# Layer 0 of a graph attention stack: putting a group's neighbour lists in order of rank on TensorE instead of through indirect transfers

## The chip, the cores and the metric

The kernel runs on one core of one Trainium2 chip. The metric is the device time of one execution in microseconds. The kernel before was run nine times; the median is 3138.7 us. The profile that the text reads is a single further execution.

## The reference

There are 3327 nodes of 256 features and a symmetric adjacency matrix with about 1% of its entries set, the diagonal included. Four layers follow one another. Each is "attention over the neighbours, added to the input, then normalised"; they differ in how the score of an edge is made. Layer 0 is the one that the change touches:

```python
g_src = nodes @ W_src_w.T + W_src_b
g_tgt = nodes @ W_tgt_w.T + W_tgt_b
g = jax.nn.leaky_relu(g_src[:, None, :] + g_tgt[None, :, :], 0.2)
score = jnp.where(adj_mat != 0, jnp.einsum('ijc,c->ij', g, a_w), -jnp.inf)
weights = jax.nn.softmax(score, axis=1)
x = layernorm(x + weights @ g_tgt)
```

Its score does not factorise: each edge needs 256 values of its own. Layers 1 to 3 have scores that are a sum of a row term and a column term, and are computed densely.

## The kernel before, in words

**Layer 0** (`sparse0`) works on the edges alone. The rows are cut into 26 tiles of 128, and the tiles into three groups of 5, 9 and 12 (`SETS`). A first stage (`targets`, lines 360 to 372) multiplies all rows with the target weights on TensorE (PE) and writes them to `table_d` in HBM, one table row per node. Beside it, and later beside the gathers, the generator `neighbours(s)` (lines 399 to 516) makes for every row of group s a list of its neighbours' table rows:

- per tile, two halves of the adjacency rows are loaded (`adj_i`, two buffers used in turn), and L425 multiplies "is an edge" with the column's number (`rev`, which holds 4096 plus the column). L448 takes the eight largest of every 104 columns, and L467 and L469 sort up to 56 of them into `found`. The tile's `payload` has 58 columns: 56 table rows, the node's own number in the group, and a mark for the diagonal.
- a key per row (number of neighbours, own number) is laid on a diagonal (L499) and spread over all partitions by a product with ones (L500, into the PSUM tile tagged "keys"). When the group's tiles are done, L509 counts for every row the keys that are larger. That is the row's rank in the group, between 0 and 128 times the group's tiles; L513 makes integers of it.

The rows of a group are then put in order of rank, so that the rows with most neighbours lie together and a tile of short rows needs fewer gathers (`LEVELS`: 56, 38, 34, 32 and 28 for the first group's five tiles). `write_list(s, t)` does this: an indirect transfer on POOL (L522) writes the 128 payloads of tile t to the places in `lists_d` that their ranks name. After the last tile `read_lists(s)` (L530) reads the list back as `lst`, where partition p of tile t holds the row of rank 128 t + p.

**The gathers.** For each sorted tile, POOL issues one indirect transfer for the nodes' own rows (L555, from `own_d`) and one per neighbour place (L563, from `table_d`), in parts of eight; a part goes into one of eleven buffers, four parts ahead of its use. DVE takes the maximum with the negated source row (L582) and sums the weighted result (L588); ACT scales the gathered rows (L669), PE adds them up (L672). L708 on POOL puts the finished rows back to their places in HBM.

**What sets the order.** In `sparse0`, PE, DVE, ACT and POOL execute in the order in which the program is written. SP's loads are not in that order: the framework's scheduler places each where it expects its buffer to be free, so loads of a later step can be issued ahead. Group 0's `neighbours` runs beside the first stage to its end; then come group 0's five `write_list`, its `read_lists`, and the loop over parts q. In this loop the `neighbours` generators of groups 1 and 2 are advanced by as many steps as their due times ask for, ahead of `score(q)` on DVE. Their list writes are put into a queue (`between`) from which POOL takes one after every second gather.

**Layers 1 to 3** (`layers`) are dense products of edge weights with features, bounded by PE. Layer 1 starts when the last group's rows are back. If some row had more neighbours than the lists hold, a flag (`lost`) would run a dense version of everything; with these inputs it does not run.

Of the kernel before, what the change touches and what calls it, by code (L numbers as in the profile page):

```python
# [8 lines left out]
F32 = mybir.dt.float32  # L9
BF16 = mybir.dt.bfloat16  # L10
I32 = mybir.dt.int32
U32 = mybir.dt.uint32
U16 = mybir.dt.uint16
AF = mybir.ActivationFunctionType
ALU = mybir.AluOpType
# [4 lines left out]
P = 128  # L20
BANK = 512
# [6 lines left out]
KMAX = 56  # L28
CHUNK = 104
FIRST = 3  # L30
BASE = 4096


SETS = (5, 9, 12)
# [13 lines left out]
def gat_stack(  # L48
# [29 lines left out]
    nc = tc.nc  # L78
    n, dim = x.shape
# [189 lines left out]
    def sparse0(lost):  # L269
        GROUP, TURNS, LEAD = 8, 11, 4  # L270
        starts = [sum(SETS[:s]) for s in range(len(SETS))]
        with ExitStack() as s0:
            const0 = s0.enter_context(tc.tile_pool(name="s_const", bufs=1))
            io0 = s0.enter_context(tc.tile_pool(name="s_io", bufs=2))
            gath = s0.enter_context(tc.tile_pool(name="gath", bufs=1))
            ps0 = s0.enter_context(tc.tile_pool(name="s_ps", bufs=2, space=PSUM))
# [21 lines left out]
            for c in range(kc):  # L298
                t = io0.tile([P, dim], F32, tag="minus", name="dots0")
# [9 lines left out]
            rev = const0.tile([P, nt * P], U16, name="rev")  # L309
# [9 lines left out]
            own_i = const0.tile([P, nt], U32, name="own_i")  # L319
# [5 lines left out]
            own_f = const0.tile([P, nt], F32, name="own_f")  # L325
# [70 lines left out]
            len_c = nt * P // CHUNK  # L396
            assert all((-(-hi // P) * P - lo) % CHUNK == 0 for lo, hi in halves)

            def neighbours(s):

                size = SETS[s]
                keys = io0.tile([P, max(SETS)], F32, tag="keys", name="keys")
                ranks = io0.tile([P, max(SETS)], F32, tag="ranks", name="ranks")
                ranks_i = io0.tile([P, max(SETS)], U32, tag="ranks_i", name="ranks_i")
                key_rows = ps0.tile([P, max(SETS) * P], F32, tag="keys", name="key_rows", bufs=1)
                payloads = []
                of_rows = iter(())
                for t in range(size):
                    it = starts[s] + t
# [6 lines left out]
                    for b, (lo, hi) in enumerate(halves):  # L416
                        w, padded = hi - lo, -(-(hi - lo) // P) * P
                        adj_i = io0.tile([P, nt * P // 2], I32, tag="adj_i", name="adj_i")
# [4 lines left out]
                        elif w < padded:  # L423
# [3 lines left out]
                            op0=ALU.not_equal, op1=ALU.mult, accum_out=sums[:pn, b : b + 1],  # L427
# [38 lines left out]
                    for r in range(0, KMAX, 8):  # L466
# [8 lines left out]
                        sums[:, 3:4], found, axis=AX.X, op=ALU.add, negate=True  # L475
                    )
                    nc.vector.tensor_reduce(lost[:, it : it + 1], sums, axis=AX.X, op=ALU.add)
                    payload = io0.tile([P, KMAX + 2], U32, tag=f"pay{t}", name="payload", bufs=1)
                    nc.vector.tensor_scalar(
                        payload[:, :KMAX], found, 1.0 - BASE, 0.0, op0=ALU.add, op1=ALU.max  # L480
                    )
                    nc.vector.tensor_copy(payload[:, KMAX : KMAX + 1], own_i[:, it : it + 1])
                    nc.vector.tensor_scalar_mul(
                        payload[:, KMAX + 1 :], sums[:, 2:3], -1.0
                    )
# [10 lines left out]
                        op0=ALU.mult, op1=ALU.subtract,  # L496
                    )
                    key_diag = io0.tile([P, P], F32, tag="key_diag", name="key_diag")
# [8 lines left out]
                for t in range(size):  # L507
# [3 lines left out]
                        op0=ALU.is_gt, op1=ALU.add, accum_out=ranks[:, t : t + 1],  # L511
                    )
                nc.vector.tensor_copy(ranks_i[:, :size], ranks[:, :size])  # L513
                placed[s] = ranks_i, payloads
                yield

            placed = {}
            listed = {}

            def write_list(s, t):  # L520
                ranks_i, payloads = placed[s]
                nc.gpsimd.indirect_dma_start(  # L522
                    out=lists_d[s][:, :],
                    out_offset=bass.IndirectOffsetOnAxis(ap=ranks_i[:, t : t + 1], axis=0),
                    in_=payloads[t][:, :], in_offset=None,
                )

            def read_lists(s):
                lst = io0.tile([P, max(SETS), KMAX + 2], U32, tag="lst", name="lst")
                nc.gpsimd.dma_start(  # L530
                    lst[:, : SETS[s], :], lists_d[s].rearrange("(t p) k -> p t k", p=P)
                )
                listed[s] = lst
# [3 lines left out]
            places = {key: LEVELS[SETS[key[0]]][key[1]] for key in tiles}  # L537
# [286 lines left out]


            first = neighbours(0)
            for it in range(nt):
                for _ in targets(it):
# [29 lines left out]
            at = begins[len(SETS) - 1]  # L858
# [3 lines left out]
            for s in range(len(SETS) - 1):  # L862
# [2 lines left out]
                    at_step(at + 2, project_next, it)  # L865
                    at += 3
                at = max(at, begins[len(SETS) - 1] + 19)
            for it in range(SETS[0]):
                write_list(0, it)
            read_lists(0)  # L870
            for s in range(1, len(SETS)):
                lo, hi = starts[s] * P, min(n, (starts[s] + SETS[s]) * P)
                copy_rows(nc.sync, own_d[s][: hi - lo, dim : 2 * dim], x[lo:hi, :])
# [3 lines left out]
            for s in range(1, len(SETS)):  # L877
                at = begins[s] - LEAD - 1
                at_step(at, read_lists, s)
                at -= SETS[s] // 4 + 1  # L880
                for it in range(SETS[s]):
                    at_step(at, between.append, lambda s=s, it=it: write_list(s, it))
                ahead.append(neighbours(s))
                steps += 6 * SETS[s] + 3
                owed[at] = steps
# [732 lines left out]
    lost = nodes.tile([P, 2 * nt], F32, name="lost")  # L1618
    nc.vector.memset(lost, 0.0)
    rest = sparse0(lost)  # L1620
    with ExitStack() as rs:
        layers(rs, EARLY, rest)
# [75 lines left out]
```

## Time and profile before

| what | us |
|---|---|
| median of nine runs (lowest, highest) | 3138.7 (3134.86, 3143.18) |
| the profiled execution's own time | 3136.12 |
| its span, first to last instruction | 3134.3 |
| first stage and group 0's ranks (to 128.8) | 128.8 |
| from there to DVE's second y operation (165.2) | 36.4 |
| from there to the end of group 1's ranks (404.6) | 239.4 |
| from there to the last put-back on POOL (1494.9) | 1090.3 |
| layers 1 to 3 (to 3134.3) | 1639.4 |

Over the whole span PE is busy 71%, DVE 72%, ACT 24%, POOL 33% of the time. From 165.2 to 404.6 us, DVE is busy for 230.9 of 239.4 us and POOL for 170.7; from 404.6 to the last gather at 1467.3, POOL for 808.7 of 1062.7 and DVE for 787.6.

A row in order of time has: start and duration in us, engine, line, operation, output<-inputs, and in brackets the idle time of the engine ahead of it with what ended it. A row of waits has: engine, what waited, its line, <- what it waited for: us in total, how many times, the longest. A group's row has: busy us, mean ns of one | idle us just before, and its releasers. "L522" is line 522 of the kernel before. [...]

### The profile page before, as it was taken

To read this page: it belongs to the slowest core of one execution; us is meant where nothing else is said; L and a number is where in the kernel's file an instruction comes from. 1 tells how busy PE (TensorE), PEld (TensorE's weight loads), DVE (VectorE), ACT (ScalarE), POOL (GpSimd) and SP (SyncE) were. 2 spreads that over 40 slices of the span, in tenths; PEclk is the share of its full clock that TensorE was granted. 3 is DMA by queue.
4 is the path that set the end of the run, shared out by engine and by line. 5 is a ranking of instruction groups with operands and counts; after the bars stand their busy time and mean duration, and the time that the engine had idled before them with its cause. 6 is when DMAs were issued, how large, how long until landed. Compare 5 with 4: busy or idle time off the path is not lost.

```text
span 3134.3 us, 44325 instructions
## 1 busy us (share of the span) xinstructions
PE 2230.1 (71%) x15676; PEld 1261.4 (40%) x15676; DVE 2260.1 (72%) x6075; ACT 750.0 (24%) x2094; POOL 1039.5 (33%) x1053
## 2 busy tenths in 40 slices
PE   7514342452443554344789999999999999999997
PEld 3302121221211221122668888884434545444332
DVE  7589999999956555554445542108888899899997
ACT  0003231432333344333234421110110110110110
POOL 0177767777777777775000000000000000000000
PEclk9998676676766776677999999999999999999998
DMA  7566546555435544443766753332212212212211
GB/s 222 155 145 188 169 124 166 171 159 150 114 101 113 133 112 117 119 116 88 226 180 201 208 151 92 105 104 73 68 45 70 68 47 69 68 45 60 56 47 47
DMA packets 179448, 367.64 MB, mean 117 GB/s; under 512 B 34294, under 2 KB 125608, under 8 KB 178194
## 3 DMA queue, kind: packets, MB, share of 16 engines
q1 hardware_dynamic: 98248, 174.31, 19.7%
q0 software_dynamic: 50688, 154.27, 18.9%
q10 hardware_dynamic: 30282, 36.15, 3.3%
q8 instruction: 126, 2.06, 0.3%
q14 instruction: 104, 0.85, 0.1%
HBM read 322.58 MB, written 45.43 MB: 117 GB/s over the span
## 4 chain that ended last, share of the span: by engine, by line
PE 45%; DVE 4%; DMA 2%; issue 1%; ACT 0%; POOL 0%; SPq 0%; DVEq 0%; POOLq 0%; ACTq 0%
PE acc L1353 17%; PE acc L1306 15%; PE acc L1361 8%; DVE e L1222 3%; PE misc L1152 3%; DMA at_i<-in_adj_t_dram 1%; DMA at<-at_d 1%; PE misc L1249 0%; PE misc L1435 0%; PE misc L1396 0%; DVE stats L1513 0%; DVE h L248 0%; DVE h L1511 0%; DVE h L1326 0%; DVE both L1508 0%
## 5 line engine op out<-in xcount | busy, mean ns | idle before, releaser
L563 POOL DMA_INDIRECT g<-table_d,lst x923 | 916.8, 993 | 281.7 <-issue 266.6
L1222 DVE SCALAR_TENSOR_TENSOR e<-rate,feat,at 128x896 f32<-128x896 f32 (+4 forms) x832 | 844.1, 1081 | 81.4 <-PE acc L1361 69.7
L672 PE MATMUL acc<-g,ident 128*128 128x512 f32 (+1 forms) x934 | 453.4, 643 | 433.8 <-ACT g L669 402.6
L1353 PE MATMUL acc<-e,feat 128*32 128x384 f32 (+2 forms) x6656 | 690.2, 516 | 7.5 <-DVE h L1326 4.8
L672 PEld LDWEIGHTS acc<-g,ident 128*128 128x128 f32 x934 | 193.2, 211 | 667.0 <-ACT g L669 445.7
L582 DVE TENSOR_TENSOR y<-g,both 128x1024 f32<-128x1024 f32 (+2 forms) x240 | 275.7, 1174 | 202.6 <-DMA g<-table_d,lst 200.3
L1353 PEld LDWEIGHTS acc<-e,feat 128*32 128x32 f32 x6656 | 258.4, 110 | 347.9 <-issue 236.0
L1361 PE MATMUL acc<-e,feat 128*32 128x384 f32 (+3 forms) x3328 | 376.0, 512 | 0.0
L669 ACT ACTIVATE g<-g,w 128x256 f32<-128x256 f32 x923 | 370.6, 493 | 0.0
L588 DVE SCALAR_TENSOR_TENSOR y<-y,both 128x256 f32<-128x256 f32 x923 | 324.7, 417 | 0.0
L1306 PE MATMUL acc<-feat,e 128*128 128x257 f32 (+2 forms) x1352 | 308.7, 384 | 21.4 <-DMA feat<-feats_d 13.3
L1306 PEld LDWEIGHTS acc<-feat,e 128*128 128x128 f32 (+2 forms) x1352 | 255.8, 192 | 63.1 <-issue 14.3
L242 POOL TENSOR_TENSOR rstds<-rstds,minus_half 128x7 f32<-128x7 f32 (+1 forms) x12 | 19.8, 1649 | 755.6 <-DVE rstds L241 755.6
L1306 PE MATMUL acc<-feat,at 128*128 128x257 bf16 (+2 forms) x2028 | 237.8, 274 | 5.2 <-DMA at<-at_d 4.9
L500 PE MATMUL key_rows<-key_diag,ones 128*128 128x128 f32 x52 | 18.0, 445 | 288.1 <-DVE key_diag L499 239.5
L1306 PEld LDWEIGHTS <-at 128*128 128x128 bf16 (+2 forms) x2028 | 198.7, 99 | 39.0 <-DMA at<-at_d 5.5
L1361 PEld LDWEIGHTS acc<-e,feat 128*32 128x32 f32 (+1 forms) x3328 | 139.0, 110 | 154.8 <-issue 131.2
L1222 DVE SCALAR_TENSOR_TENSOR e<-rate,feat,at_i 128x896 f32<-128x896 f32 (+2 forms) x104 | 111.3, 1080 | 95.8 <-ACT feat L1160 54.3
L1202 POOL DMA_DIRECT2D rate3b_d<-rate_rows x4 | 2.1, 520 | 468.0 <-ACT rate_rows L1201 468.0
L448 DVE MAX8 cand<-num 128x8 f32<-128x104 uint16 x832 | 145.6, 251 | 1.0
L500 PEld LDWEIGHTS key_rows<-key_diag,ones 128*128 128x128 f32 x52 | 11.9, 278 | 301.6 <-DVE key_diag L499 223.2
L1239 ACT CAST at<-at_i 128x896 bf16<-128x896 int32 (+2 forms) x104 | 92.0, 885 | 98.6 <-DMA at_i<-in_adj_t_dram 70.7
(182 smaller groups left out, 1758.5 us busy)
## 6 DMA issues: line engine op xcount, KB each, us to landing
at<-at_d SPq DMA_DIRECT2D x150, 224.0 KB, 2.5
at_i<-in_adj_t_dram SPq DMA_DIRECT2D x50, 448.0 KB, 4.9
adj_i<-in_adj_dram SPq DMA_DIRECT2D x25, 832.0 KB, 4.6
adj_i<-in_adj_dram SPq DMA_DIRECT2D x25, 831.5 KB, 5.3
g<-table_d,lst POOLq DMA_INDIRECT x923, 2.8
at<-at_d SPq DMA_DIRECT2D x75, 192.0 KB, 2.4
at<-at_d SPq DMA_DIRECT2D x75, 191.8 KB, 2.3
at_d<-at ACTq DMA_DIRECT2D x50, 224.0 KB, 4.1
```

The costliest lines, as they stand in the source:

```text
L448: nc.vector.max(cand[:, lo // CHUNK + c, :], spread_v[:, c, :, :])
L563: nc.gpsimd.indirect_dma_start(out=g[:, k - k0, :], out_offset=None, in_=table_d[:, :], in_offset=bass.IndirectOffsetOnAxis(ap=entry["lst" ...
L582: nc.vector.tensor_tensor(y, rows, minus_src[:, None, :].to_broadcast([P, m, dim]), op=ALU.max)
L588: nc.vector.scalar_tensor_tensor(y, y, 1.0, a, op0=ALU.mult, op1=ALU.mult, accum_out=sc)
L669: nc.scalar.activation(rows, rows, AF.Copy, scale=w[:, k : k + 1])
L672: nc.tensor.matmul(dst, ident, rows, start=start, stop=stop)
L1152: nc.tensor.matmul(pacc[:pn, : dim + self.extra], ht[:, k, :pn], self.weight[:, k, :], start=(k == 0), stop=(k == kc - 1),)
L1222: nc.vector.scalar_tensor_tensor(e[:pn, : c1 - c0], self.rate[b][:pn, h_of, : c1 - c0], q, at[:pn, : c1 - c0], op0=ALU.max, op1=ALU.mult,)
L1239: nc.scalar.copy(at[:pn, :w], at_i[:pn, :w])
L1306: nc.tensor.matmul(accs[s][:pn, : dim + 1], a[:pj, s * P : s * P + pn], f[:pj, : dim + 1], start=(j == 0 and part == 0), stop=(j == nt - 1 ...
L1353: nc.tensor.matmul(accs[x][p][q : q + 32, : hi - lo], f[:pj, at0 : at0 + 32], es[at0 // hd][:pj, lo:hi], start=(j == 0), stop=(j == nt - 1),)
L1361: nc.tensor.matmul(accs[x][pairs][h_of * 32 : (h_of + 1) * 32, : hi - lo], f[:pj, dim + h_of : dim + h_of + 1].to_broadcast([pj, 32]), es[ ...
```

## The change

For group 0 alone, the sorted list is made on chip. `neighbours(0)` calls a new function, `permute`, behind the rank count; the five L522 transfers of group 0 and their L530 read are gone. Groups 1 and 2 keep theirs. The payloads of group 0 are float32 instead of uint32.

`permute` splits every rank into a tile number (rank shifted right by 7) and a row (rank minus 128 times that), and adds 4096 to both, so that they can be compared with `rev`. For each of the five tiles it makes a 128x128 matrix with a 1 where the row's place is the column ("unit"), a 5-wide mark of the tile ("pick"), and the payload repeated five times and multiplied with the mark ("moving", 5 x 58 = 290 columns, in the buffers tagged "adj_i"). A product of unit and moving, added up over the five tiles in one PSUM bank (tagged "keys"), has the list in order of rank; one copy makes integers of it.

```diff
+            placed = {}
+            listed = {}
+
             def neighbours(s):
...
-                    payload = io0.tile([P, KMAX + 2], U32, tag=f"pay{t}", name="payload", bufs=1)
+                    payload = io0.tile(
+                        [P, KMAX + 2], U32 if s else F32, tag=f"pay{t}", name="payload", bufs=1
+                    )
...
-                    nc.vector.tensor_copy(payload[:, KMAX : KMAX + 1], own_i[:, it : it + 1])
+                    nc.vector.tensor_copy(payload[:, KMAX : KMAX + 1], own_f[:, it : it + 1])
...
                 nc.vector.tensor_copy(ranks_i[:, :size], ranks[:, :size])
                 placed[s] = ranks_i, payloads
+                if s == 0:
+                    permute(size, ranks, ranks_i, payloads)
                 yield
 
-            placed = {}
-            listed = {}
+            def permute(size, ranks, ranks_i, payloads):
+
+
+                at = io0.tile([P, 2, max(SETS)], F32, tag="places", name="places", bufs=1)
+                tile_i, tile_f, row_f = ranks_i[:, :size], at[:, 0, :size], at[:, 1, :size]
+                nc.vector.tensor_scalar(
+                    tile_i, tile_i, 7, None, op0=ALU.logical_shift_right
+                )
+                nc.vector.tensor_copy(tile_f, tile_i)
+                nc.vector.scalar_tensor_tensor(
+                    row_f, tile_f, -float(P), ranks[:, :size], op0=ALU.mult, op1=ALU.add
+                )
+
+                nc.vector.tensor_scalar(
+                    at[:, :, :size], at[:, :, :size], float(BASE), None, op0=ALU.add
+                )
+                cols = size * (KMAX + 2)
+                assert cols <= BANK and n >= P
+                sorted_ps = ps0.tile([P, max(SETS) * P], F32, tag="keys", name="sorted", bufs=1)
+                for t in range(size):
+                    unit = io0.tile([P, P], F32, tag="key_diag", name="unit")
+                    nc.vector.tensor_scalar(
+                        unit, rev[:, :P], row_f[:, t : t + 1], None, op0=ALU.is_equal
+                    )
+                    pick = io0.tile([P, max(SETS)], F32, tag="keys", name="pick")
+                    nc.vector.tensor_scalar(
+                        pick[:, :size], rev[:, :size], tile_f[:, t : t + 1], None, op0=ALU.is_equal
+                    )
+                    moving = io0.tile(
+                        [P, size, KMAX + 2], F32, tag="adj_i", name="moving"
+                    )
+                    nc.vector.tensor_tensor(
+                        moving, payloads[t][:, None, :].to_broadcast([P, size, KMAX + 2]),
+                        pick[:, :size, None].to_broadcast([P, size, KMAX + 2]), op=ALU.mult,
+                    )
+                    nc.tensor.matmul(
+                        sorted_ps[:, :cols], unit, moving.rearrange("p t k -> p (t k)"),
+                        start=(t == 0), stop=(t == size - 1),
+                    )
+                lst = io0.tile([P, max(SETS), KMAX + 2], U32, tag="lst", name="lst")
+                nc.vector.tensor_copy(
+                    lst[:, :size, :].rearrange("p t k -> p (t k)"), sorted_ps[:, :cols]
+                )
+                listed[0] = lst
...
                 at = max(at, begins[len(SETS) - 1] + 19)
-            for it in range(SETS[0]):
-                write_list(0, it)
-            read_lists(0)
             for s in range(1, len(SETS)):
                 lo, hi = starts[s] * P, min(n, (starts[s] + SETS[s]) * P)
```

## The prediction, on record before the result

> **What bounds the kernel now.** I read the page's costliest groups first, then the waits of POOL and DVE over the whole run, then both engines' rows in order of time around the change.
>
> ```profile
> L563 POOL DMA_INDIRECT g<-table_d,lst x923 | 916.8, 993 | 281.7 <-issue 266.6
> ```
>
> Layer 0 is a stream of 923 gathers on POOL. Busy and idle together are some 1,200 us of the 1,314 between the first gather (153.5 us) and the last (1467.3), and the idle time is issue (0.30 us ahead of each). So the time of layer 0 is when the stream starts, plus its length, plus whatever stops it. Two of POOL's waits over the whole run name what stops it:
>
> ```profile
> POOL lists_d L522 <- DVE ranks_i L513: 123.9, 1, 123.9
> ...
> POOL lists_d L522 <- DVE lost L610: 20.3, 1, 20.3
> POOL lists_d L522 <- DMA lists_d<-payload,ranks_i: 14.9, 6, 4.3
> ```
>
> The first is the start (group 0 has to be ranked). The second is a stop in mid-stream. In order of time, POOL at both places:
>
> ```profile
> 129.19 2.43 POOL L522 DMA_INDIRECT lists_d<-payload,ranks_i  x1 [123.86 <-DVE ranks_i L513]
> 135.61 1.09 POOL L522 DMA_INDIRECT lists_d<-payload,ranks_i  x1 [3.99 <-DMA lists_d<-payload,ranks_i]
> ...
> 148.34 0.93 POOL L530 DMA_DIRECT2D lst<-lists_d  x1 [1.53 <-DMA lists_d<-payload,ranks_i]
> 152.22 1.00 POOL L555 DMA_INDIRECT own_of<-own_d,lst  x1 [2.94 <-DMA lst<-lists_d]
> ...
> 162.28 0.94 POOL L563 DMA_INDIRECT g<-table_d,lst  x1 [0.30 <-issue]
> ...
> 404.85 0.98 POOL L522 DMA_INDIRECT lists_d<-payload,ranks_i  x1 [20.26 <-DVE lost L610]
> ```
>
> The six transfers to be removed fill 129.19 to 152.22. But at 404.85 POOL has stood still for 20.26 us, waiting for group 1's ranks from DVE. Whatever POOL gains before that point is lost there, unless DVE is earlier too. So DVE's stretch from group 0's ranks (128.72) to group 1's (404.40) decides:
>
> ```profile
> 128.72 0.17 DVE L513 CAST ranks_i<-ranks 128x5 uint32<-128x5 f32 x1
> 128.80 1.88 DVE L425 SCALAR_TENSOR_TENSOR num<-adj_i,rev 128x1664 uint16<-128x1664 int32 x1
> ...
> 156.94 0.42 DVE L582 TENSOR_TENSOR y_own<-own_of,both 128x256 f32<-128x256 f32 x1 [18.26 <-ACT both L579]
> ...
> 160.24 1.22 DVE L582 TENSOR_TENSOR y<-g,both 128x1024 f32<-128x1024 f32 x1 [2.82 <-DMA g<-table_d,lst]
> 165.17 1.22 DVE L582 TENSOR_TENSOR y<-g,both 128x1024 f32<-128x1024 f32 x1 [3.71 <-DMA g<-table_d,lst]
> ...
> 404.40 0.17 DVE L513 CAST ranks_i<-ranks 128x9 uint32<-128x9 f32 x1
> ```
>
> DVE does the first tile of group 1 at once (128.80 to 138.69), then waits 18.26 + 2.82 + 3.71 = 24.8 us for the first gathers, all of it before 165.17. From 165.17 to 404.40 the list of DVE's waits is empty. So what the change is worth is how much earlier the row at 165.17 comes. After 404.85 nothing stops POOL until its last rows, and the next layer begins with its last one (1492.49).
>
> One more thing is seen in time: a gather caught by L425 is stretched.
>
> ```profile
> 203.35 2.44 POOL L563 DMA_INDIRECT g<-table_d,lst  x1 [0.30 <-issue]
> ```
>
> L425 ran on DVE from 203.09 to 204.98, and the gather ended 0.8 us later. All 41 POOL transfers over 1.4 us lie beside one of the 42 L425 rows after 128 us in this way.
>
> **What the Trainium skill says.** "SBUF — State Buffer", section "Who interferes with whom": a DVE instruction with two SBUF inputs holds the port pair that it shares with GpSimd. L425 reads adj_i and rev from SBUF; the trace agrees (0.95 us becomes 2.44). "DMA: Bandwidth & Descriptors", section "Anatomy of one DMA": about 2 us of a transfer are fixed, most of it the receipt of the write. The list writes landed after 2.2 us (median), though the first took over 4 beside two adjacency loads. "TensorE: Matmul & The Clock Gate", section "What's actually happening": an idle array starts at half clock. Here four 128x256 instructions take 1.91 us after 48.89 us of idling as after 3.41, so my price, taken from these rows, holds that already. For the widened multiply see the next part.
>
> **The change, part by part.**
>
> *Removed*: five L522 writes, the L530 read. POOL's 129.19 to 152.22 (23.0 us) is free.
>
> *Added before the first product* (DVE): shift, cast, fused multiply-add, base added: four small ones, dependent, 0.19 us apart as L463 and L464 are: from 128.91 to 129.67. Then the unit matrix (128x128, as L499: 0.29, next one after 0.21), the pick (128x5) and the product with it, which waits some 0.19 for the pick. This last, 128x290 with two SBUF inputs, the trace does not have; "VectorE: DVE Perf Modes", section "The TRN2 errata", gives (N+151)/0.96 ns, so 0.46 us as an estimate (the same formula gives 1.22 for 128x1024, and the row above has 1.22). The first product can start at about 130.65.
>
> *Added on PE*: five f32 products of 290 columns, two instructions each. Instructions of 128 columns start 0.28 us apart, of 256 0.46 to 0.50, of 260 0.51; carried on to 290 columns 0.51 to 0.56, so 1.02 to 1.13 for a product, and I take 1.1. DVE needs 0.8 for the next tile's three operations, so PE sets the pace: 5.5 us and 0.2 to drain, end 136.35. Bounds: 0.8 (DVE's pace) and 1.5 us (double the 674 ns mean of L351's 260 columns, and a tenth more): the end moves by -1.5 to +2.
>
> *Copy of the sorted list* from PSUM: L509 took 0.88 for 640 columns, so 0.5 for 290: 136.9. POOL starts 0.3 later, as at 129.19: **own_of at 137.2 instead of 152.22, 15.0 earlier.** Late next could be own_d and table_d, which the gathers read: their last writes are issued at 120.79 and 117.63 and land in 2.6 us (median), before 137. No wait there.
>
> *Moved: group 1's first adjacency loads.* The moving tiles take the two "adj_i" buffers in turn, five uses after ten loads and two index rows. So the loads for tile 0 of group 1, which SP had issued at 109.72 and 119.68, wait for the fourth and fifth product: issued at about 135.35 and 136.4. Such a load landed 5.3 us after its issue at 77.40, so the first is there at 140.65; the second, even at twice that, before 147. Behind them on SP are only loads that are later still. DVE's first tile, which had run from 128.80, now runs at 140.65, 3.7 us after the copy; its halves take 5.17 and 4.72: 150.54. Then y_own, y at 151.1, and the second y could go at 152.3.
>
> *The gathers meanwhile*: 1.25 us each from 137.2, but both L425 rows (140.65 and 145.85) now catch one, and cost about 1.5 each: the ninth POOL transfer (at 162.28 before) starts at 137.2 + 8 x 1.25 + 2.9 = 150.1, and as before 2.89 us pass until DVE's second y: **153.0 instead of 165.17, 12.2 earlier**. By DVE alone 12.9. If the loads were not late, the collisions would come earlier and the gathers would still say about 153. So the two limits lie close together, and 12.2 is what I take.
>
> *Cost at nothing*: 20 DVE and 10 PE instructions, covered by time in which both stood idle; without that cover 8 us, what is between 128.8 and 136.9. The payload's type and its own-number copy: same shapes.
>
> *After that*: DVE's stretch to 404.40 holds no wait, so group 1's ranks come 12.2 earlier; POOL arrives earlier too, waits its 20 us, and goes on from the same event, so their relative places afterwards are the same. Sum: 3136.1 (profiled execution; span 3134.3) - 12.2 = 3123.9. The median of the nine is 3138.7, 2.6 above that execution: **3138.7 - 12.2 = 3126.5**.
>
> **The rivals.** (a) *The lead is swallowed*: POOL's 20.26 us wait simply grows to 35, time 3138.7. For: it is on the same engine, and DVE is busy throughout before it. Against: the 24.8 us that DVE waits before 165.17 are in the same stretch. (b) *Adjacency late*: SP takes a column load (xt) first, which waits for the products behind the sorting ones on PE (some 3 us), and the two loads share the way with the gathers, 2 us more: 7 us gained, 3131.7. For: the first stage moves 209 GB/s; against: SP has served such loads by readiness. (c) *Slower*: after 404.85 POOL is the bound and 24 of its transfers are caught by L425, 23.2 us in all, 0.97 each (0.54 to 1.70 by row). If the new phase made them all 1.70, 17.6 us would be added: 3144.1. It decides from 12.2/24 more, 1.48 a piece. Against: both engines start again from one event. (d) *The list is late anyway*, because products with 290 columns take twice what I take: 5.5 later, 3132.0.
>
> **How the numbers follow.** Forecast 0.74 (3122 to 3130), (a) 0.07, (b) and (d) together 0.12, (c) 0.07. Range 3122 to 3133: the first case and most of (b) and (d). A measurement of this kernel can tell some 0.2% from no change, 6.3 us: 3132.4 to 3145.0. Faster 0.82 (the first case and two thirds of (b) and (d)), same 0.12, slower 0.06 (what lies beyond (c)).
>
> **What would show it.** Right: own_of at about 137 on POOL; the first L425 of group 1 waiting for adj_i until about 141; the second y at about 153; then no DVE wait until ranks at 392; POOL's L522 wait still about 20 us; its last row near 1480. Wrong: a DVE wait between 153 and 392; products over 1.3 us; a stop on POOL after 392; or a changed length of the layers after 1495 (1,639 us).

## The result, and the profile after

The kernel with the change takes 3126.88 us (median of nine runs, 3123.07 to 3130.82). The kernel before took 3138.7 in the same comparison (29 runs, 3134.51 to 3143.18): ratio 0.9963, 95% interval 0.9955 to 0.9971, so 11.8 us less. The forecast was 3126.5. The profiled execution of after took 3123.54 (span 3121.6), against 3136.12 (3134.3) of before: 12.7 us less in the span. Lines are those of after from here on: 49 more than before behind the new function (L522 is L571, L555 is L604, L563 is L612, L582 is L631), three to five more ahead of it (L425 is L428, L513 is L518).

The profile's costliest group and, from POOL's waits over the whole run, the two that take the place of the two shown of before:

```profile
L612 POOL DMA_INDIRECT g<-table_d,lst x923 | 923.7, 1001 | 283.1 <-issue 263.1
```

```profile
POOL own_of L604 <- DVE lst L564: 131.7, 1, 131.7
...
POOL lists_d L571 <- DVE lost L659: 17.8, 1, 17.8
```

The stream of 923 gathers is still the bulk of layer 0. (A gather's row on POOL is not its transfer: it takes 1.0 us on the mean, while the data land 2.8 us after the issue.) What released the stream's start is now the copy of the sorted list on DVE, at 137 us. The wait for group 1's ranks is still there, 17.8 us instead of 20.3. POOL in order of time at these places, and at its last put-back:

```profile
137.02 1.06 POOL L604 DMA_INDIRECT own_of<-own_d,lst  x1 [131.70 <-DVE lst L564]
138.38 0.98 POOL L612 DMA_INDIRECT g<-table_d,lst  x1 [0.30 <-issue]
139.67 2.59 POOL L612 DMA_INDIRECT g<-table_d,lst  x1 [0.30 <-issue]
...
145.08 2.35 POOL L612 DMA_INDIRECT g<-table_d,lst  x1 [0.30 <-issue]
...
392.88 0.99 POOL L571 DMA_INDIRECT lists_d<-payload,ranks_i  x1 [17.76 <-DVE lost L659]
...
1483.49 0.97 POOL L757 DMA_INDIRECT sums_d<-hs,lst  x1 [17.87 <-DVE hs L750]
```

The last put-back of the kernel before:

```profile
1492.49 0.97 POOL L708 DMA_INDIRECT sums_d<-hs,lst  x1 [17.38 <-DVE hs L701]
```

There are three different gains: `own_of` starts 15.2 us earlier than before (152.22), group 1's first write 12.0 earlier (404.85), the last put-back 9.0 earlier (1492.49). The two rows of 2.59 and 2.35 us are gathers caught by L428 (the rows at 139.53 and 144.71 below). DVE in the same stretch:

```profile
128.70 0.17 DVE L518 CAST ranks_i<-ranks 128x5 uint32<-128x5 f32 x1
128.91 0.17 DVE L529 TENSOR_SCALAR ranks_i<-ranks_i 128x5 uint32<-128x5 uint32 x1
...
130.19 0.46 DVE L555 TENSOR_TENSOR moving<-payload,pick 128x290 f32<-128x290 f32 x1
...
136.26 0.46 DVE L564 CAST lst<-sorted 128x290 uint32<-128x290 f32 x1 [0.85 <-PE sorted L559]
139.53 1.89 DVE L428 SCALAR_TENSOR_TENSOR num<-adj_i,rev 128x1664 uint16<-128x1664 int32 x1 [2.81 <-DMA adj_i<-in_adj_dram]
...
144.71 1.89 DVE L428 SCALAR_TENSOR_TENSOR num<-adj_i,rev 128x1663 uint16<-128x1663 int32 x1
...
149.73 1.21 DVE L631 TENSOR_TENSOR y<-g,both 128x1024 f32<-128x1024 f32 x1
153.25 1.22 DVE L631 TENSOR_TENSOR y<-g,both 128x1024 f32<-128x1024 f32 x1 [2.31 <-DMA g<-table_d,lst]
...
392.43 0.17 DVE L518 CAST ranks_i<-ranks 128x9 uint32<-128x9 f32 x1
```

The 24.8 us in which DVE waited are now 2.81 for the moved adjacency load and 2.31 for the gathers. (Its waits for PE inside the sorting, 2.0 us in all, count as sorting below.) And the products on PE, behind a wait for the first moving tile:

```profile
130.80 4.22 PE L559 MATMUL sorted<-moving,unit 128*128 128x290 f32 x8 [6.29 <-DVE moving L555]
135.47 0.76 PE L559 MATMUL sorted<-moving,unit 128*128 128x290 f32 x2 [0.45 <-DVE moving L555]
136.06 1.03 PE L351 MATMUL pss<-w_src,xt 128*128 128x256 f32 x4
```

Four products (eight instructions) in 4.22 us are 1.06 each; the last one, which DVE held up by 0.45, took 0.76.

### The profile page after: what moved, and what is told of

The parts are those of the page before. It is cut to its first block, busy times and chain, and to the rows that moved or that the text cites. A ratio compares the mean times of both kernels' runs of the same rounds, so it can differ in the third digit from the quotient of the medians.

```text
span 3121.6 us, 44357 instructions
## 1 busy us (share of the span) xinstructions
PE 2233.3 (72%) x15686; PEld 1261.5 (40%) x15686; DVE 2265.4 (73%) x6095; ACT 750.2 (24%) x2094; POOL 1040.2 (33%) x1047
## 3 DMA queue, kind: packets, MB, share of 16 engines
q1 hardware_dynamic: 98248, 174.31, 19.7%
## 4 chain that ended last, share of the span: by engine, by line
PE 45%; DVE 4%; DMA 2%; issue 1%; ACT 0%; POOL 0%; ACTq 0%; SPq 0%; DVEq 0%; POOLq 0%
PE acc L1399 17%; PE acc L1352 15%; PE acc L1407 9%; DVE e L1268 3%; PE misc L1198 3%; DMA at<-at_d 1%; DMA at_i<-in_adj_t_dram 1%; PE misc L1295 0%; PE misc L1481 0%; PE misc L1442 0%; DVE h L248 0%; DVE stats L1559 0%; DVE h L1557 0%; DVE h L1372 0%; DMA h<-sums_d 0%
## 5 line engine op out<-in xcount | busy, mean ns | idle before, releaser
L612 POOL DMA_INDIRECT g<-table_d,lst x923 | 923.7, 1001 | 283.1 <-issue 263.1
L631 DVE TENSOR_TENSOR y<-g,both 128x1024 f32<-128x1024 f32 (+2 forms) x240 | 275.7, 1174 | 201.0 <-DMA g<-table_d,lst 186.0
L505 PEld LDWEIGHTS key_rows<-key_diag,ones 128*128 128x128 f32 x52 | 11.9, 278 | 279.3 <-DVE key_diag L504 250.5
```

Source lines behind the costliest of these rows:

```text
L612: nc.gpsimd.indirect_dma_start(out=g[:, k - k0, :], out_offset=None, in_=table_d[:, :], in_offset=bass.IndirectOffsetOnAxis(ap=entry["lst" ...
L631: nc.vector.tensor_tensor(y, rows, minus_src[:, None, :].to_broadcast([P, m, dim]), op=ALU.max)
```

## The experiments

**The theory**: the gain is the idle time that the change takes out of DVE's stretch from group 0's ranks to group 1's, less the work it puts in; POOL waits at its end in any case. **The rivals**: POOL's earlier start counts by itself; or the five writes and the read are not the cause.

The first four kernels ran on one chip, where the kernel before took 3138.13 (27 runs, 3134.82 to 3142.61).

### 1. Buffers of their own for the moving tiles

```diff
-                        [P, size, KMAX + 2], F32, tag="adj_i", name="moving"
+                        [P, size, KMAX + 2], F32, tag="moving", name="moving"
```

> The changed kernel with the five moving tiles in two buffers of their own, so that group 1's first adjacency loads are issued ahead again. Theory (the gathers of the first part set DVE's second y, and L425 holds up two of them wherever it falls): DVE's wait for adj_i of 2.8 us goes, but the two collisions only come earlier, the second y stays at 153 +-0.7, time 3126.9 +-1.5. Rival (the lost prefetch costs what DVE waited): second y at about 150.5, time 3124.1.

Measured: 3123.05 (3122.06 to 3126.5), ratio 0.9959, interval 0.9946 to 0.9973. POOL's first row, and DVE:

```profile
137.69 2.43 POOL L604 DMA_INDIRECT own_of<-own_d,lst  x1 [132.37 <-DVE lst L564]
```

```profile
137.31 1.88 DVE L428 SCALAR_TENSOR_TENSOR num<-adj_i,rev 128x1664 uint16<-128x1664 int32 x1
...
153.42 1.22 DVE L631 TENSOR_TENSOR y<-g,both 128x1024 f32<-128x1024 f32 x1 [2.38 <-DMA g<-table_d,lst]
```

The wait for adj_i is gone: the first L428 starts at 137.31. Yet the second y starts at 153.42 and group 1's ranks come at 392.56, as in after (153.25, 392.43). The collisions only came earlier (`own_of` took 2.43, a gather at 142.97 2.23), and the gathers set the second y. So the wait of 2.81 us for the load costs nothing, as the prediction had it ("the gathers would still say about 153"). The median alone would have favoured the rival (3124.1 expected by it, 3126.9 +-1.5 by the theory): it lies 3.8 below after's. But the two intervals overlap, and the last put-back comes at the same time (1483.50 here, 1483.49 there), so this is not counted as a gain.

### 2. The same, and two more steps of group 1 ahead of the first score

```diff
-                for _ in range(goal):
+                for _ in range(goal if q else goal + 2):
```

This takes the place of DVE's wait for the gathers with work that is owed anyway.

> As own_buffers, and two more steps of group 1's first tile (its sort and its key, 6.5 us of DVE work that use no gathered row) ahead of the first score. Theory (group 1's ranks on DVE set the time, so DVE time idle before the second y is what counts): the second y at about 155 instead of 153.25, but 6.5 us of work less behind it, group 1's ranks 4.9 us earlier, at about 387.5; POOL's wait there falls from 17.8 to about 13; time 3122. Rival (what counts is when POOL starts to gather, which is the same): 3126.9.

Measured: 3120.13 (3117.99 to 3121.05), ratio 0.9946, interval 0.9933 to 0.996; against kernel 1, the same but for the steps, 2.9 less. The two intervals overlap, but the runs themselves do not (3117.99 to 3121.05 here, 3122.06 to 3126.5 there). DVE in order of time:

```profile
146.34 0.21 DVE L456 COPY few<-cand 128x96 f32<-128x96 f32 x1
...
153.07 0.41 DVE L631 TENSOR_TENSOR y_own<-own_of,both 128x256 f32<-128x256 f32 x1
...
153.46 2.34 DVE L631 TENSOR_TENSOR y<-g,both 128x1024 f32<-128x1024 f32 x2
...
387.05 0.17 DVE L518 CAST ranks_i<-ranks 128x9 uint32<-128x9 f32 x1
```

No row has a bracket: DVE now goes on with group 1 at 146.34, and when it comes to y, both gathers are there. Group 1's ranks are 5.4 us earlier than in after, POOL's wait is 11.51 instead of 17.76, though POOL started at the same time (136.80 against 137.02). That speaks against the first rival. This kernel is the fastest of all: 18.0 us below the kernel before of the same comparison, where the change alone had 11.8 in its own.

### 3. Group 1's first steps behind the first score

```diff
-                for _ in range(goal):
+                for _ in range(goal if q else 0):
```

> The changed kernel with group 1's first tile (9.9 us on DVE) not ahead of the first score but spread over the later parts. Theory (DVE's stretch to group 1's ranks): no collisions at the start, second y at about 150, but 9.9 us more to do behind it: ranks 6.7 us later, near 399; time 3133.6. Rival (POOL's stream sets the time; its first gathers are 2.8 us sooner): 3124.

Measured: 3132.72 (21 runs, 3129.91 to 3134.85), ratio 0.9983, interval 0.9977 to 0.999: 5.8 more than after. DVE again:

```profile
145.20 0.42 DVE L631 TENSOR_TENSOR y_own<-own_of,both 128x256 f32<-128x256 f32 x1 [8.83 <-ACT both L628]
...
149.72 1.22 DVE L631 TENSOR_TENSOR y<-g,both 128x1024 f32<-128x1024 f32 x1 [2.54 <-DMA g<-table_d,lst]
...
153.94 1.89 DVE L428 SCALAR_TENSOR_TENSOR num<-adj_i,rev 128x1664 uint16<-128x1664 int32 x1
...
398.39 0.17 DVE L518 CAST ranks_i<-ranks 128x9 uint32<-128x9 f32 x1
```

Here the gathers run undisturbed and the second y comes 3.5 us *earlier* than in after, but DVE has idled 11.7 us ahead of it instead of 5.1, and its group 1 work begins only at 153.94. The ranks come 6.0 later. So the second y, by which the prediction measured, tells the gain only where the same work lies ahead of it; the idle time tells it in any case.

### 4. The kernel before, with six more steps ahead of the first score

The edit is that of kernel 2 with 6 in place of 2, made to the kernel before: no permutation, the six transfers stay.

> The kernel before, list writes and all, with six more steps of group 1's neighbours (16.5 us of DVE work) ahead of the first score, in the 18 us in which DVE waited for the first gathers. Theory (the change gained DVE's idle time and nothing else): group 1's ranks some 14 to 16 us earlier, POOL's wait there down from 20 to 4 to 6, though its first gather still starts at 152 to 154; time about 3123.5, as good as the change. Rival (the gathers' start counts): 3138.7.

Measured: 3129.66 (3120.98 to 3130.77), ratio 0.9971, interval 0.996 to 0.9982. POOL and DVE (line numbers of the kernel before):

```profile
152.20 0.93 POOL L530 DMA_DIRECT2D lst<-lists_d  x1 [4.56 <-DMA lists_d<-payload,ranks_i]
158.13 1.00 POOL L555 DMA_INDIRECT own_of<-own_d,lst  x1 [5.00 <-DMA lst<-lists_d]
...
392.76 0.98 POOL L522 DMA_INDIRECT lists_d<-payload,ranks_i  x1 [2.67 <-DVE lost L610]
```

```profile
162.92 0.42 DVE L582 TENSOR_TENSOR y_own<-own_of,both 128x256 f32<-128x256 f32 x1 [7.98 <-ACT both L579]
...
171.03 1.22 DVE L582 TENSOR_TENSOR y<-g,both 128x1024 f32<-128x1024 f32 x1 [3.49 <-DMA g<-table_d,lst]
...
392.31 0.17 DVE L513 CAST ranks_i<-ranks 128x9 uint32<-128x9 f32 x1
```

The gathers start 5.9 us *later* than before, and the kernel is 8.5 faster: group 1's ranks come 12.1 earlier, 10.4 of them because DVE idles 14.4 us instead of 24.8. POOL's wait for them is down to 2.67 us, so its late start is all but used up. The size was missed by 6 us. Two to four of them lie ahead of the ranks, which were to come 14 to 16 earlier: the last list write and the read of the list landed late (waits of 4.56 and 5.00, before 1.53 and 2.94), beside adjacency loads that the added steps had brought forward. Two more lie behind the ranks (2732.0 us from there to the end, before 2729.9); the rest is not located. Six steps of other work thus give most of what the permutation gives.

These four and the two kernels in one sum, each from its own DVE rows: group 1's ranks, less group 0's, less the sorting stretch (L529 to the end of L564), less the idle time for adj_i, both and g.

| kernel | group 0's ranks | sorting | idle | group 1's ranks | rest |
|---|---|---|---|---|---|
| before | 128.72 | 0 | 24.79 | 404.40 | 250.9 |
| after | 128.70 | 7.81 | 5.12 | 392.43 | 250.8 |
| 1, own buffers | 128.80 | 8.40 | 4.63 | 392.56 | 250.7 |
| 2, and two steps | 128.41 | 7.90 | 0 | 387.05 | 250.7 |
| 3, no steps | 128.35 | 7.81 | 11.65 | 398.39 | 250.6 |
| 4, before and six steps | 128.26 | 0 | 14.38 | 392.31 | 249.7 |

The rest is the same within 0.3 us in five of them; why it is 1.1 less in kernel 4 is not known. So the change's 12.0 us at group 1's ranks are 19.7 of idle time taken out and 7.8 of sorting put in.

### 5. The permutation, and the five writes and the read kept on POOL

```diff
+                    ranks_c = io0.tile([P, max(SETS)], U32, tag="ranks_c", name="ranks_c", bufs=1)
+                    nc.vector.tensor_copy(ranks_c[:, :size], ranks[:, :size])
+                    placed[s] = ranks_c, payloads
...
+            kept_d = dram.tile([SETS[0] * P, KMAX + 2], F32, name="kept_d")
+            for it in range(SETS[0]):
+                nc.gpsimd.indirect_dma_start(
+                    out=kept_d[:, :],
+                    out_offset=bass.IndirectOffsetOnAxis(ap=placed[0][0][:, it : it + 1], axis=0),
+                    in_=placed[0][1][it][:, :], in_offset=None,
+                )
+            kept = io0.tile([P, max(SETS), KMAX + 2], F32, tag="kept", name="kept", bufs=1)
+            nc.gpsimd.dma_start(
+                kept[:, : SETS[0], :], kept_d.rearrange("(t p) k -> p t k", p=P)
+            )
```

> The changed kernel, but the five list writes of group 0 and the read stay on POOL ahead of its gathers (to a table and a tile that nothing uses; the sorted list still comes from the products). Theory: what the change removed is this time on POOL's queue, and the products only replace its result; own_of starts at about 149 (POOL need not wait for the read to land), the second y comes at about 162, group 1's ranks 3 us earlier than before at most, time 3136. Rival (the gain lies elsewhere, in lighter traffic or another order on SP): 3127.

It ran on another chip, where the kernel before took 3589.73 (56 runs, 3569.15 to 3623.86): 3588.2 (22 runs), ratio 0.9993, interval 0.9974 to 1.0011. POOL:

```profile
144.04 0.96 POOL L922 DMA_INDIRECT kept_d<-payload,ranks_c  x1 [5.82 <-DMA kept_d<-payload,ranks_c]
148.78 0.93 POOL L928 DMA_DIRECT2D kept<-kept_d  x1 [3.78 <-DMA kept_d<-payload,ranks_c]
150.01 0.99 POOL L607 DMA_INDIRECT own_of<-own_d,lst  x1 [0.30 <-issue]
```

```profile
162.93 1.22 DVE L634 TENSOR_TENSOR y<-g,both 128x1024 f32<-128x1024 f32 x1 [3.59 <-DMA g<-table_d,lst]
```

The list is sorted by PE, but POOL comes to `own_of` only at 150.01, and the second y is at 162.93. With the six transfers back no gain is left that the time shows. The interval is 13 us wide and has room for up to 9 us of gain; and the plain change did not run on this chip, only three kernels that hold it and more work, whose times were all shorter than before (below). The early rows say it more surely than the time: counted as in the table above, DVE idles 13.5 us there and sorts for 8.7, 22.1 together where the kernel before has 24.8. With the rest unchanged, 2.6 of the 12.0 us that the change gained at group 1's ranks would be left.

### 6. Slack of POOL and DVE: inconclusive

Two loads, each at an early and a late place, were to measure what a later POOL or DVE costs ahead of group 1's ranks and ahead of group 2's: eight gathers into a spare tile (8 x 1.25 = 10 us of POOL) at part 4 or 26, or five maxima of 936 columns (1.14 us each on DVE) at part 4 or 30. What they make is not used.

```diff
+                if q == 4:
+                    for k in range(8):
+                        nc.gpsimd.indirect_dma_start(
+                            out=spare[:, k % 4, :], out_offset=None, in_=table_d[:, :],
+                            in_offset=bass.IndirectOffsetOnAxis(
+                                ap=listed[0][:, 0, k : k + 1], axis=0
+                            ),
+                        )
```

```diff
+                if q == 4:
+                    for _ in range(5):
+                        nc.vector.max(spare, rev[:, :936])
```

> The changed kernel with eight more gathers on POOL (rows of the first tile once more, into a tile that nothing reads; 10 us at 1.25) in group 0's stream. Theory: POOL has 17.8 us to spare ahead of group 1's ranks; its wait there falls to about 7.7, time 3126.9 +-1.5. Rival (POOL's stream sets the time from its start): 3136.9.

> The same eight gathers behind group 1's ranks, at the first part of group 1. Theory and rival: POOL has no wait from there to its last row, so all 10 us are seen: 3136.9. Only if DVE alone set the pace to group 2's ranks as well would part of it be hidden.

> The changed kernel with five more DVE operations (maximum over 936 16-bit values, about 1.03 us each, 5.1 us in all[...]) at part 4, between the second y and group 1's ranks. Theory: nothing on DVE waits there, so ranks come 5.1 us later and the time is 3132.0. Rival (POOL's stream): 3126.9.

> The same five DVE operations behind group 1's ranks, at part 30. Theory: group 2's ranks are ready at 844.9 and POOL asks for them at 846.5, so DVE has 1.6 us to spare there, and 3.5 of the 5.1 us are seen: 3130.4, with a wait of about 3.5 us on POOL's first list write of group 2. Rival (POOL alone sets the time after group 1's ranks): 3126.9.

These four met a chip on which the kernel before took 3567.59 (11 runs, 3550.47 to 3583.49). Ratios: gathers early 0.9917 (0.9873 to 0.9961), late 0.9878 (0.9829 to 0.9928); DVE early 0.9883 (0.9843 to 0.9922), late 0.9848 (0.9812 to 0.9885). Three were run again, on the chip of experiment 5:

> The changed kernel with eight more gathers on POOL (rows of the first tile once more, into a tile that nothing reads; 10 us at 1.25) in group 0's stream. Theory: POOL has 17.8 us to spare ahead of group 1's ranks; its wait there falls to about 7.7, time as without them (3126.9 +-2). Rival (POOL's stream sets the time from its start): 10 us more, 3136.9.

> The same eight gathers behind group 1's ranks, at the first part of group 1. Theory and rival: POOL has no wait from there to its last row, so all 10 us are seen: 3136.9. If DVE set the pace up to group 2's ranks instead, part of it would be hidden.

> The changed kernel with five more DVE operations (maximum over 936 16-bit values, some 5.1 us in all[...]) behind group 1's ranks, at part 30. Theory: group 2's ranks are ready at 844.5 and POOL asks for them at 846.5, so DVE has 2 us to spare there, and 3 of the 5.1 us are seen: 3130, with a wait of about 3 us on POOL's first list write of group 2. Rival (POOL alone sets the time after group 1's ranks): 3126.9.

Ratios 0.9916 (0.989 to 0.9942), 0.9845 (0.9809 to 0.9881) and 0.9895 (0.986 to 0.993). On both chips POOL has stops of up to 25 us in the gather stage that the profiles of the first chip lack, and group 1's first write comes at 462 to 521 us instead of 393. POOL stands for 24.0 us ahead of it in all seven, with the eight gathers ahead of it or without, so this wait doesn't show them either. The runs of one kernel lie up to 79 us apart, and the effects looked for are 5 to 10 us; nothing about slack follows, except that all seven hold the change and lie below the kernel before. Why they lie so far below it, and the kernel of experiment 5 does not, is not known.

## Why the prediction was right, step by step

- **Start of the first product**: 130.65 predicted, 130.80. The multiply of 290 columns took 0.46 as estimated from the Trainium skill, "VectorE: DVE Perf Modes", section "The TRN2 errata".
- **The products**: 1.1 us each and the end at 136.35 predicted; 1.06 for four, 0.76 for the last, and the copy starts at 136.26. `own_of` was to start at 137.2 and did at 137.02. This is in part luck: PE did not set the pace alone, since DVE waited for it (0.66 and 0.46 us) and it then for DVE (0.45), and the faster last product made up for that. In kernel 1, where all five were slow, the copy started at 136.94. Rival (d) did not occur.
- **The moved adjacency load**: issue at 135.35, landed at 140.65 predicted. SP's row of the two loads starts at 135.06, and L428 starts at 139.53: the landing was 1.1 us less late than priced. Rival (b) did not occur. Kernel 1 shows that the wait is free.
- **The two caught gathers**: 1.5 each predicted, 1.6 and 1.4 (2.59 and 2.35 against 0.96). The second y was to start at 153.0 and did at 153.25, 11.9 earlier.
- **DVE to group 1's ranks**: no wait, as predicted; they come 12.0 earlier.
- **POOL's wait**: about 20 predicted, 17.76. Of the 2.5 us, some 1.4 are a slower step: group 0's gathers, where nothing catches them, start 1.259 us apart on the mean, 1.250 before, and there are about 160. The rest is the caught ones: 18 of them, longer by 23.0 us in all, before 16 by 18.7; the prediction had two more at 1.5. Since POOL waits here, it costs nothing. Rival (a), which had this wait grow to 35, fell with it.
- **After group 1's ranks**: "their relative places afterwards are the same" is the step that did not hold to the microsecond. From the ranks to the last put-back it takes 1091.1 us (1483.49 - 392.43), before 1088.1 (1492.49 - 404.40). The collisions did not do it: 22 rows over 1.4 us with 23.2 us in all, before 24 rows with 23.2; so rival (c) did not occur. Kernels 1 to 3 have 1090.9 each, kernel 4, without the change, 1089.4. Of the 3.0 us, 0.4 lie ahead of group 2's first write, 1.8 between it and the last gather, 0.8 behind that. About half is a slower step again (from one gather to the next, 1.255 and 1.254 us in groups 1 and 2, before 1.253 and 1.252).
- **Layers 1 to 3**: unchanged length predicted. From the start of the last put-back to the end it is 1638.1 us, before 1641.8 (the 1639 of the prediction count from 1494.9, some 2.4 us later): 3.7 less, one of the signs named for being wrong. It falls at two places, both in code that the change doesn't touch: 1.7 between one row norm on POOL and the next write of rates there (from 571.1 to 619.4 us after the put-back; before, 571.4 to 621.4), and 1.6 after the last row norm (11.7, before 13.3). Kernels 1 to 3 have the same two (47.5 to 48.7, and 11.7 to 11.8), kernel 4 has those of before (50.0 and 13.4).

So the span's 12.7 us are 12.0 - 3.0 + 3.7. The mechanism was right, and each term of DVE's path up to group 1's ranks within 1.2 us; but that the total came out within 0.4 us of the forecast owes something to luck: two unpredicted terms all but cancel, and the medians differ by 11.8 where the two profiled executions differ by 12.6.

**What stays open**: why the gathers' step is some ns longer in after and in kernels 1 to 3 (over all three groups it is 1.255 us in these four, 1.252 in before and in kernel 4, and 1.254 to 1.258 in the eight profiles on the other two chips, which all hold the permutation); what shortens the two places of layers 1 to 3; how much slack there is before group 2's ranks. There, DVE's ranks come at 844.54 and POOL's first write at 846.46, so DVE is only some 2 us ahead; in kernel 2 (840.61 and 841.15) POOL takes them almost at once. From that point DVE would be the bound again, and experiment 6 was to show it.

## What to carry to other kernels

Find the wait that stops the bounding stream, and the engine that ends it: a faster path is worth the idle time it takes out of that engine's stretch less the work it puts in (19.7 - 7.8 here), not what it takes out of the queue (23.0) or how much earlier the stream starts (15.2). Then ask whether owed work can fill the same idle time: reordering alone gave 8.5 us here without the new path, and on top of it group 1's ranks came 5.4 earlier again.

## What the runs showed of the hardware that was not expected

- **PE became faster during the sorting, and not in 60 us of work before it.** The fifth product took 0.76 us against 1.06, and the four 128x256 instructions behind it 1.03, where those ahead of group 0's ranks in the kernel before took 1.91. The trace's record of the granted clock first rises 3.7 us after the first product here, and 6.6 us after it in kernel 1. The Trainium skill, "TensorE: Matmul & The Clock Gate", Part 1 ("The HAM clock gate"), puts the change of clock some 4 us into sustained work, give or take half a microsecond. The sorting products agree with that only roughly, and the first stage does not: from 60 to 120 us the profile has PE busy for 60.0 of 60.0 us, and four 128x260 instructions take 2.10 us at 61.73 as at 107.21. What makes the difference is not shown.
- **A lower mean clock that is no slower clock.** The mean granted clock is 0.853 in after and 0.872 in before. The record begins with its first rise, at 134.5 us in after and at 265.9 in before, and the mean counts what lies ahead of it as full speed.
- **A list read of the same size landed in under 3 us or in 5.** In kernel 4 the wait for it was 5.00 us beside adjacency loads, in before 2.94; for the last list write 4.56 against 1.53.
- **The same kernel took 3138, 3568 and 3590 us.** The first is that of the first two comparisons, the others were measured on two other chips: a difference more than thirty times what the change is worth. Each of the two was measured at one time only, so whether it is the chip or the time is not shown.
